# Way in to a batch's experts, an early norm, and silu by tanh in a two-layer Mamba and mixture-of-experts kernel

## The chip, the cores and the metric

The kernel runs on one core of one Trainium2 chip. The metric is the device time of one execution in microseconds (us), as a median over runs. A second set of numbers comes from one execution that was recorded by the hardware profiler.

## The reference

The input is 4 batches of 512 tokens with 256 features. Two layers follow, each a mixer and a mixture of experts. Each of the four parts takes the layernorm of its input and adds the layernorm of its result.

```python
x = x + ln(L0_attn(ln(x)))   # Mamba2-like mixer, 32 heads, state 64, chunks of 128,
                             # then a gated feed-forward of 1024: silu(h @ gate.T) * (h @ up.T) @ down.T
x = x + ln(L0_ffn(ln(x)))    # top 2 of 8 experts, relu(x @ fc)**2 @ proj, weighted by softmax
x = x + ln(L1_attn(ln(x)))   # X = silu(conv(x @ in.T)), gate = sigmoid(x @ g.T), dt = softplus(X . dt_w + dt_b)
                             # s = scan(exp(dt * A), dt * B * X); out = ((C * s + D * X) * gate) @ out.T
x = x + ln(L1_ffn(ln(x)))    # scores = sigmoid(x @ gate.T); top 2 of 8 (scores + bias); xs = score * x in bf16
                             # sum over e: (silu(xs @ w1[e].T) * (xs @ w3[e].T)) @ w2[e].T, plus a shared expert
```

In layer 0 the feed-forward has an RMS norm of its own (norm2) and a residual inside L0_attn. Layer 1's silu stands in three places: behind the conv of the mixer, in the shared expert, and in the eight routed experts.

## The kernel before

Everything runs in one launch. The tokens of a batch are four chunks of 128 (`NC`), and the tiles are 128 partitions high. There are two phases.

In the first, a loop over the batches runs layer 0's mixer, eight head groups for each batch. Beside it, a helper `Side` gives out steps of earlier batches' work. `side.go(us, done)` is called at points of the mixer with the time passed since the last call, and lets the helper run steps of batches before `done` until a share of 0.62 of that time is used. The steps come from generators: `layer0(b)` is the feed-forward of batch b (`feed_forward`) and, for batches 0 and 1, the way into its experts (`experts0_in`), the experts (`experts0_out`) and the way back (`experts0_back`). `side.finish()` behind the loop issues all that is left, one step after the other.

In the second phase new pools are opened, among them buffers of psum: tag `dc` has two of two banks, tag `b` has two. Work is cut into lanes: last feed-forward (of batch 3), `experts0_in`, `experts0_out`, `experts0_back` (for batches 2 and 3), then `mixer1_in`, `mixer1_out`, `experts1_in` and `experts1_out` for all four. A planner picks the next step among the lanes by costs that the steps yield (`yield pe, dve, latency`) and by a rank of the batches, `[2, 3, 0, 1]`. The order that it finds is the program order on each engine, and each engine executes its own in order.

The parts that the change and the steps of the prediction touch, with lines of the kernel before:

- `normed` (L285): RMS norm of a batch by four ACT copies with a scale into `v`, then transposes into `vT` (L135, L139).
- `last_feed_forward`: eight slices of the hidden 1024. Gate and up matmuls (L1003), tanh on ACT (L1005), two DVE steps into `hf` (L1006, L1007), down matmuls (L1012). This one already computes silu as 0.5 * g * (1 + tanh(g / 2)).
- `experts0_in`: layernorm, a copy of the batch to DRAM, transposes into `xT`, router matmuls (L245), top 2 on DVE, counting matmuls (L359, L361) that sort the token slots by expert, places (L380), matmuls that give the tokens of each tile (L403), token numbers (L408) and rows of weights.
- `experts0_out`: 15 tiles (`NT`) of 128 sorted slots. `fetch` gathers tokens `xr` (L441) and expert weights `wx` (L444) by indirect DMAs on POOL's queue, and `three` works on three tiles at a time: transposes of `xr` (L452), first matmul (L459), relu on ACT (L462), square on DVE, second matmul (L467), copy to `yr` (L470), and its DMA to DRAM.
- `experts0_back`: eight gathers on POOL's queue (L494) bring each token's two results back, and ACT and DVE add them up.
- `mixer1_in`: matmul with `w1i` (L1054), conv in four terms (L199 on ACT, L201 on DVE), silu on ACT in place (L1058), gate matmuls and tanh (L1064, L1065), dt as softplus by exp and ln (L209, L212).
- `mixer1_out`: dt rows by DMA, product `uu` on POOL (L1092), exp (L1093) and X times D (L1094) on ACT, scan and two more DVE steps (L1097 to L1099), output matmuls (L1102).
- `experts1_in`: norm, router, top 2 and scores `s`, then the shared expert by `gated` (L1114 matmuls, L1116 silu on ACT, L1117 product on DVE).
- `experts1_out`: for each of four chunks and two halves of the experts, matmuls into a buffer `gu` of tag `dc` (L1164), four silus on ACT with the token's score as scale (L1169), four products on DVE into `he` (L1172). Then transposes (L1183), copies, and the second matmuls with the final layernorm.

The half of `experts1_out` in code:

```python
sg = wk.tile([P, L], F32, tag="s2b", name="sg", bufs=2)
for i in range(4):
    e, o = half * 4 + i, i * P
    S.activation(sg[:, o : o + P], gu[:, o : o + P], AF.Silu, scale=s[:, c, e : e + 1])
for i in range(4):
    e, o = half * 4 + i, i * P
    V.scalar_tensor_tensor(he[:, e, :], gu[:, L + o : L + o + P], s[:, c, e : e + 1],
                           sg[:, o : o + P], ALU.mult, ALU.mult)
```

ACT holds the table of one set of functions at a time; where the next function is of another set, an ACT_TABLE_LOAD stands ahead of it, under the line of that function. In the kernel before, exp (L422) and tanh (L1005) follow each other without one (871.64 and 874.67 us), and silu, exp and ln are each led by one.

Of the kernel before, what the change touches and what calls it, by code (L numbers as in the profile page):

```python
# [37 lines left out]
def tile_layers(  # L38
# [234 lines left out]

    def normed(b, v, vT):

        h1 = h1s[b]
        mv = stats(h1, "a")
        q = small.tile([P, NC], F32, tag="q", name="q")  # L280
        V.tensor_tensor(q, mv[:, :, 0], mv[:, :, 0], ALU.mult)
        V.tensor_tensor(q, q, mv[:, :, 1], ALU.add)
        r = rsqrt(q, "rsa")
        for c in range(NC):
            S.activation(v[:, c, :], h1[:, c, :], AF.Copy, scale=r[:, c : c + 1])  # L285
        yield 0.0, 2.6, 4.0
        transposed(vT, [v[:, c, :] for c in range(NC)], lambda k: cv("norm2", k), "dc")
        yield 1.0, 0.0, 1.8

    def feed_forward(b, beside=True):  # L290

        h1 = h1s[b]
        v = wl.tile([P, NC, DM], F32, tag="v", name="v", bufs=1)
        vT = wl.tile([P, 2, L], F32, tag="vT", name="vT", bufs=1)
        yield from normed(b, v, vT)
        for half in range(2):
            hs, wds = [], []
            for f in range(half * 4, half * 4 + 4):
                we = wst.tile([P, 8, P], F32, tag="wx", name="wf", bufs=5)
                nc.sync.dma_start(out=we[:, 0:2, :], in_=w_gate[:, :, f * P : (f + 1) * P])  # L300
                nc.sync.dma_start(out=we[:, 2:4, :], in_=w_up[:, :, f * P : (f + 1) * P])
                wd = we[:, 4:6, :].rearrange("p a c -> p (a c)")
                nc.sync.dma_start(out=wd, in_=w_down[:, f, :])
                gu = ps("dc", 2)
                gp, up = gu[:, :L], gu[:, L:]
                for i, p in enumerate((gp, up)):
                    for k in range(2):
                        T.matmul(p, we[:, i * 2 + k, :], vT[:, k, :], start=(k == 0), stop=(k == 1))  # L308
                th = wl.tile([P, L], F32, tag="th", name="th", bufs=2)
                S.activation(th, gp, AF.Tanh, scale=0.5)  # L310
                V.scalar_tensor_tensor(th, th, 1.0, gp, ALU.add, ALU.mult)
                hT = wl.tile([P, L], F32, tag="hT", name="hT", bufs=5)
                V.scalar_tensor_tensor(hT, th, 0.5, up, ALU.mult, ALU.mult)  # L313
                hs.append(hT)
                wds.append(wd)
                yield 3.44, 1.5, 0.0
            for c2 in range(2):
                acc = ps("dc", 2)[:, :L]
                for i in range(2):
                    c = c2 * 2 + i  # L320
                    for f in range(4):
                        T.matmul(acc[:, i * DM : (i + 1) * DM], hs[f][:, c * P : (c + 1) * P], wds[f],
                                 start=(f == 0), stop=(f == 3))
                h = h1[:, c2 * 2 : c2 * 2 + 2, :]
                V.tensor_tensor(h, h, rows(acc), ALU.add)
                yield 3.44, 0.7, 0.0
        yield 0.0, 0.0, 0.5
        if beside:
            yield from add_layernorm_by_chunks(b, [h1[:, c, :] for c in range(NC)])
        else:  # L330
            add_layernorm(b, [h1[:, c, :] for c in range(NC)], "a")
        yield 0.0, 4.5, 2.0

    def experts0_in(b, t):
# [8 lines left out]
        V.tensor_copy(lg, router(xT, wr, "dc"))  # L343
        yield 1.8, 0.3, 0.0
        m1, o1 = top1(lg, small, "taa")
        if b < 2:
            yield 0.0, 1.5, 0.3
        l2 = small.tile([P, NC, 8], F32, tag="tla", name="tl")
        V.scalar_tensor_tensor(l2, o1, -3e38, lg, ALU.mult, ALU.add)
        m2, o2 = top1(l2, small, "tba")  # L350
        hot = small.tile([P, NC, 8], BF16, tag="hot", name="hot", bufs=1)
        V.tensor_tensor(hot, o1, o2, ALU.add)
        yield 0.0, 1.9 if b < 2 else 3.4, 0.3

        p = ps("dc", 2)
        sums = p[:, : 5 * 64].rearrange("p (c a e) -> p c a e", a=8, e=8)
# [5 lines left out]
        for c in range(NC):  # L362
# [28 lines left out]
        tl = small.tile([P, 2 * NC, NT], F32, tag="tl15", name="tl15", bufs=1)  # L391
        V.tensor_tensor(tl, partf[:, 1].unsqueeze(2).to_broadcast([P, 2 * NC, NT]),
                        lane[:, :NT].unsqueeze(1).to_broadcast([P, 2 * NC, NT]), ALU.is_equal)
        if b < 2:
            yield 0.0, 1.9, 0.3
        tk = small.tile([P, 2 * NC, 2, NT], BF16, tag="tk", name="tk", bufs=1)
        V.tensor_scalar(tk[:, :, 0, :], tl, mine, None, ALU.mult)
# [109 lines left out]
    def layer0(b, t):  # L507

        yield from feed_forward(b)
        if b < 2:  # L510
            yield from experts0_in(b, t)
            yield from experts0_out(b, t, 0.0)


# [1 line left out]
    with ExitStack() as c1:  # L516
# [369 lines left out]
        for b in range(B):  # L886
# [78 lines left out]
                V.tensor_tensor(h0[:, c2 * 2 : c2 * 2 + 2, :], h0[:, c2 * 2 : c2 * 2 + 2, :], rows(p), ALU.add)  # L965
            side.go(2.0, b + 1)
            t = ahead
        side.finish()


# [4 lines left out]
    def last_feed_forward(b):  # L975
# [9 lines left out]

        wes = [load(f) for f in range(2)]
        yield 0.0, 0.0, 0.0
        v = wl.tile([P, NC, DM], F32, tag="v", name="v", bufs=1)
        vT = wk.tile([P, 2, L], F32, tag="vTf", name="vT", bufs=1)
        yield from normed(b, v, vT)  # L990
        acc = ps("o", 2)
        pend = []
        for f in range(9):
# [43 lines left out]


    D1 = w2.tile([P, 4], F32, tag="D1", name="D1")
    V.tensor_scalar_mul(BC, BC, 0.5)  # L1040
    V.tensor_scalar_mul(D1, col[:, OFF["D1"] : OFF["D1"] + 4], 0.5)

    def mixer1_in(b, t):
        xn = wk.tile([P, NC, DM], F32, tag="xn", name="xn", bufs=2)
        layernorm(b, "m", xn)
        yield 0.0, 2.8, 4.0
        xT = wk.tile([P, 2, L], F32, tag="xTb", name="xT1", bufs=1)
        turned(xT, xn, "b")
        yield 1.0, 0.0, 1.8
        t.X = X = wk.tile([P, 4, L], F32, tag="X", name="X", bufs=2)  # L1050
        for m in range(4):
            p = ps("b")
            for k in range(2):
                i = T.matmul(p, w1i[:, k, m * P : (m + 1) * P], xT[:, k, :], start=(k == 0), stop=(k == 1))  # L1054
                if b + m + k == 0:
                    later(i)
            conv(X[:, m, :], p, lambda t, m=m: cv("cw1", m * 4 + t), cv("cb1", m))
            S.activation(X[:, m, :], X[:, m, :], AF.Silu)  # L1058
            yield 1.72, 2.3, 0.0, (5 if m == 3 else 0)
        t.Gt = Gt = wk.tile([P, 4, L], F32, tag="Gt", name="Gt", bufs=1)  # L1060
        for m in range(4):
            p = ps("b")
            for k in range(2):
                T.matmul(p, w1g[:, k, m * P : (m + 1) * P], xT[:, k, :], start=(k == 0), stop=(k == 1))  # L1064
            S.activation(Gt[:, m, :], p, AF.Tanh, scale=0.5)  # L1065
            yield 1.72, 0.0, 0.0
        dp = ps("b").rearrange("p (c a h) -> p c a h", a=16, h=8)
        for c in range(NC):
            for m in range(4):
                T.matmul(dp[:, c], X[:, m, c * P : (c + 1) * P], repeated(dtw[:, m, :], 16),  # L1070
                         start=(m == 0), stop=(m == 3))
# [37 lines left out]
    def gated(dst, w1, w3, rhs):  # L1109
# [3 lines left out]
            for k in range(2):  # L1113
                T.matmul(p, w[:, k, :], rhs[:, k, :], start=(k == 0), stop=(k == 1))  # L1114
        sg = wk.tile([P, L], F32, tag="s2b", name="sg", bufs=2)
        S.activation(sg, gp, AF.Silu)  # L1116
        V.tensor_tensor(dst, sg, up, ALU.mult)  # L1117

    we1 = {}

# [5 lines left out]
    def experts1_in(b, t):  # L1126
# [8 lines left out]
        t.xb = wk.tile([P, 2, L], BF16, tag="xb", name="xb", bufs=2)  # L1135
        V.tensor_copy(t.xb, xT)
        yield 1.0, 0.7, 1.8
        sc = small.tile([P, NC, 8], F32, tag="lg1", name="sg")
        S.activation(sc, router(xT, fg, "dc"), AF.Tanh, scale=0.5)
        V.tensor_scalar(sc, sc, 0.5, 0.5, ALU.mult, ALU.add)  # L1140
        sel = small.tile([P, NC, 8], F32, tag="sel", name="sel")
        V.tensor_tensor(sel, sc, fb.unsqueeze(1).to_broadcast([P, NC, 8]), ALU.add)
        _, o1, _, o2 = top2(sel, small, "e")
        V.tensor_tensor(o1, o1, o2, ALU.add)
        t.s = small.tile([P, NC, 8], F32, tag="s1", name="s1")
        V.tensor_tensor(t.s, o1, sc, ALU.mult)
        yield 1.8, 4.5, 0.5, 7
        t.hs = wk.tile([P, L], F32, tag="hs", name="hs", bufs=1)
        gated(t.hs, sw1, sw3, xT)
# [1 line left out]

    def experts1_out(b, t):

        xb, s, hs = t.xb, t.s, t.hs
        fw1, fw3, fw2, sw2 = (we1[n] for n in ("fw1", "fw3", "fw2", "sw2"))
        hes = {}

        def inner(c):
            hes[c] = he = wk.tile([P, 8, P], BF16, tag="he", name="he", bufs=3)
            for half in range(2):  # L1160
# [5 lines left out]
                sg = wk.tile([P, L], F32, tag="s2b", name="sg", bufs=2)  # L1166
                for i in range(4):
                    e, o = half * 4 + i, i * P
                    S.activation(sg[:, o : o + P], gu[:, o : o + P], AF.Silu, scale=s[:, c, e : e + 1])  # L1169
                for i in range(4):  # L1170
                    e, o = half * 4 + i, i * P
                    V.scalar_tensor_tensor(he[:, e, :], gu[:, L + o : L + o + P], s[:, c, e : e + 1],  # L1172
                                           sg[:, o : o + P], ALU.mult, ALU.mult)
                yield 1.0, 1.0, 1.4

        def outer(c2):

# [31 lines left out]

    held1 = [Held() for _ in range(B)]
    none = lambda b: iter(())
    stages = [lambda b: last if b == B - 1 else none(b)]
    stages += [lambda b, f=f: f(b, held1[b]) if b > 1 else none(b) for f in (experts0_in, experts0_out, experts0_back)]
    stages += [lambda b, f=f: f(b, held1[b]) for f in (mixer1_in, mixer1_out, experts1_in, experts1_out)]
    N = len(stages)
    rank = [2, 3, 0, 1]
# [123 lines left out]
```

## Time and profile before

| | |
|---|---|
| median of 9 runs | 1286.13 us |
| lowest and highest | 1278.35 and 1294.2 us |
| profiled execution | 1281.69 us |
| its span | 1280.0 us |
| granted TensorE clock | 0.961 of full |
| busy: PE, weight load, DVE, ACT, POOL | 1110.8, 691.7, 793.7, 546.1, 325.3 us |
| ACT_TABLE_LOADs | 63, of 1283 ns each |
| of these before 851 us, 851 to 1061, after 1061 | 25, 11, 27 |

The engines are PE (TensorE's matmuls, with its weight loads apart as PEld), DVE (VectorE), ACT (ScalarE), POOL (GpSimd) and SP (SyncE, which issues DMAs only). A timeline's row gives start, duration, engine, line, operation, output and inputs with their shape, a count, and in brackets the idle time ahead of it with the engine and tile that ended it. A group's row gives a line, the operation, the count, then the busy time, the mean of one in ns, and idle time before.

The last mixer's matmuls end near 860 us. The last feed-forward's gate and up matmuls start at 870.85 us, and it ends at 922.07. From about 1061 us on only layer 1 is left.

### The profile page before, as it was taken

Reading aid. Unit: us, or ns where it says so; the run is one execution under the profiler, and the core shown is the slowest. Engines: PE = TensorE matmul, PEld = TensorE weight load, DVE = VectorE, ACT = ScalarE, POOL = GpSimd, SP = SyncE. Lnnn points to the kernel's source line nnn. Section 1 sums busy time; section 2 is a strip of 40 time slices with the busy share of each in tenths; the row PEclk is TensorE's granted clock in tenths of the full one; section 3 lists DMA queues with packets and bytes.
Section 4 is the critical chain, followed back from the end, with each engine's and each line's share of the span. In section 5 each row is a group of like instructions: output and inputs, shape, how many; then the busy total and the mean of one; then the engine's idle time right before and its main releaser. Section 6 shows DMA issues by size and latency. Waiting matters only on the chain. (4 is left out here: it accounts for less than half of the span.)

```text
span 1280.0 us, 18525 instructions
## 1 busy us (share of the span) xinstructions
PE 1110.8 (87%) x6896; PEld 691.7 (54%) x6896; DVE 793.7 (62%) x1742; ACT 546.1 (43%) x984; POOL 325.3 (25%) x411
## 2 busy tenths in 40 slices
PE   4788888999889899999889999978987697887876
PEld 3344544556546665556556665645656474554543
DVE  6568766656776564767774556743361654876765
ACT  2343432333344434333335433222254556786644
POOL 5021202001214432211134322123234833120200
PEclk9999999999899999999999999989999897999888
DMA  5011010011105453110125440145256552010100
GB/s 157 20 51 34 17 35 18 17 54 34 34 18 166 126 161 108 43 37 19 51 80 157 140 149 25 38 122 176 82 172 185 145 161 74 1 50 1 43 17 25
DMA packets 76153, 97.41 MB, mean 76 GB/s; under 512 B 11008, under 2 KB 62208, under 8 KB 76064
## 3 DMA queue, kind: packets, MB, share of 16 engines
q0 software_dynamic: 13488, 45.10, 12.1%
q1 hardware_dynamic: 53936, 43.26, 11.4%
q10 hardware_dynamic: 8640, 7.87, 1.8%
q8 instruction: 55, 0.90, 0.3%
q14 instruction: 34, 0.28, 0.1%
HBM read 85.25 MB, written 12.12 MB: 76 GB/s over the span
## 5 line engine op out<-in xcount | busy, mean ns | idle before, releaser
L540 PE MATMUL ps_pj<-uT,wg 128*128 128x512 f32 x512 | 256.8, 626 | 9.4 <-ACT bt L698 4.1
L201 DVE SCALAR_TENSOR_TENSOR BT<-ps_pj,col,BT 128x511 f32<-128x511 f32 (+2 forms) x192 | 143.4, 747 | 110.9 <-ACT BT L199 107.5
L719 POOL TENSOR_SCALAR_AFFINE_SELECT sc<-sc 128x1024 f32<-128x1024 f32 x64 | 69.9, 1092 | 460.4 <-DVE sc L716 452.8
L201 DVE SCALAR_TENSOR_TENSOR CT<-ps_pj,col,CT 128x511 f32<-128x511 f32 (+2 forms) x192 | 142.6, 743 | 20.7 <-ACT CT L199 18.1
L540 PEld LDWEIGHTS ps_pj<-uT,wg 128*128 128x128 f32 x512 | 90.6, 194 | 96.1 <-issue 72.3
L199 ACT ACTIVATE CT<-ps_pj,col 128x512 f32<-128x512 f32 x64 | 49.7, 777 | 118.4 <-PE ps_pj L540 118.4
L713 PEld LDWEIGHTS ps_dc<-CT,BT 64*128 64x128 f32 x1024 | 71.0, 190 | 46.5 <-issue 29.3
L713 PE MATMUL ps_dc<-CT,BT 64*128 64x128 f32 x1024 | 89.5, 294 | 7.6 <-DVE sc L716 6.0
L716 DVE TENSOR_TENSOR sc<-sc,ps_dc 128x1024 f32<-128x1024 f32 x64 | 77.7, 1214 | 23.9 <-PE ps_dc L713 21.2
L308 PE MATMUL ps_dc<-vT,wf 128*128 128x512 f32 x192 | 87.9, 597 | 0.7 <-DVE hT L313 0.7
L199 ACT ACTIVATE BT<-ps_pj,col 128x512 f32<-128x512 f32 x64 | 49.7, 776 | 82.9 <-PE ps_pj L540 82.9
L444 POOL DMA_INDIRECT wx<-in_w_exp_dram,wrow x60 | 59.4, 989 | 87.3 <-PE ps_dc L467 38.4
L708 ACT ACTIVATE sc<-ps_dc 128x1024 f32<-128x1024 f32 x64 | 65.6, 1025 | 37.1 <-PE ps_dc L705 36.7
L467 PE MATMUL ps_dc<-wx,hx 128*128 128x256 f32 x240 | 64.8, 395 | 12.5 <-ACT hx L462 11.1
L459 PEld LDWEIGHTS ps_dc<-hx,wx 128*128 128x128 f32 x480 | 61.0, 191 | 18.3 <-issue 9.6
L441 POOL DMA_INDIRECT xr<-XD,token x60 | 58.7, 979 | 42.8 <-PE ps_dc L452 26.9
L459 PE MATMUL ps_dc<-hx,wx 128*128 128x128 f32 x480 | 64.9, 278 | 4.7 <-DMA wx<-in_w_exp_dram,wrow 2.7
L698 ACT COPY bt<-ps_pj 128x384 f32<-128x384 f32 x64 | 30.5, 476 | 77.4 <-PE ps_pj L696 77.4
L463 DVE TENSOR_TENSOR hx<-hx 128x256 f32<-128x256 f32 x60 | 27.4, 458 | 56.7 <-ACT hx L462 56.6
L467 PEld LDWEIGHTS ps_dc<-wx,hx 128*128 128x128 f32 x240 | 43.3, 192 | 30.7 <-ACT hx L462 17.5
L308 PEld LDWEIGHTS ps_dc<-vT,wf 128*128 128x128 f32 x192 | 35.3, 190 | 40.6 <-issue 38.6
L730 PEld LDWEIGHTS ps_pj<-xd,bt 128*128 128x128 f32 x384 | 46.5, 191 | 16.3 <-issue 7.8
(315 smaller groups left out, 2005.9 us busy)
## 6 DMA issues: line engine op xcount, KB each, us to landing
wg<-in_w_in_dram SPq DMA_DIRECT2D x64, 256.0 KB
YS<-yr ACTq DMA_DIRECT2D x60, 128.0 KB
wf<-in_w_gate_dram SPq DMA_DIRECT2D x32, 128.0 KB
wf<-in_w_up_dram SPq DMA_DIRECT2D x32, 128.0 KB
wf<-in_w_down_dram SPq DMA_DIRECT2D x32, 128.0 KB
db<-dD SPq DMA_DIRECT2D x32, 128.0 KB
St<-Mv SPq DMA_DIRECT2D x192, 2.0 KB
x<-in_x_dram SPq DMA_DIRECT2D x4, 512.0 KB
```

What stands on the lines that cost most here:

```text
L199: S.activation(dst, p, AF.Identity, bias=bias, scale=w(3))
L201: V.scalar_tensor_tensor(dst[:, s:], p[:, : L - s], w(3 - s), dst[:, s:], ALU.mult, ALU.add)
L308: T.matmul(p, we[:, i * 2 + k, :], vT[:, k, :], start=(k == 0), stop=(k == 1))
L441: keep(G.indirect_dma_start(out=xr[t], out_offset=None, in_=x, in_offset=bass.IndirectOffsetOnAxis(ap=token[:, t : t + 1], axis=0)))
L444: keep(G.indirect_dma_start(out=ws[t], out_offset=None, in_=w_exp, in_offset=bass.IndirectOffsetOnAxis(ap=wrow[:, t : t + 1], axis=0)))
L459: T.matmul(p[:, L + d * P : L + (d + 1) * P], w[:, k * DM + d * P : k * DM + (d + 1) * P], h[:, k * P : (k + 1) * P], start=(k == 0), stop ...
L467: T.matmul(p[:, 2 * P : 2 * P + DM], h[:, (2 + d) * P : (3 + d) * P], w[:, (2 + d) * DM : (3 + d) * DM], start=(d == 0), stop=(d == 1))
L540: T.matmul(p, w[:, k, :], uT[:, k, :], start=(k == 0), stop=(k == 1))
L708: S.activation(sc, df, AF.Exp)
L713: T.matmul(cb[:, e * L + c * P : e * L + (c + 1) * P], of.BT[e * 64 : (e + 1) * 64, c * P : (c + 1) * P], of.CT[e * 64 : (e + 1) * 64, c * ...
L716: V.tensor_tensor(sc, sc, cb, ALU.mult)
L719: G.affine_select(out=scv, in_=scv, compare_op=ALU.is_ge, fill=0.0, base=0, pattern=[[0, 2 * NC], [1, P]], channel_multiplier=-1)
```

## The change

It has three parts.

1. The way into batch 2's experts (`experts0_in(2)`) is now in `layer0(2)`, behind its feed-forward, among the steps that `side` gives out. It leaves the planner's lanes.
2. `normed` is cut in two. `scaled(b)` holds the statistics and the four ACT copies into `v`. For batch 3 it is issued at once behind the mixer's loop, ahead of `side.finish()`; the transposes stay where they were.
3. In layer 1, silu(g) is computed as 0.5 * g * (1 + tanh(g / 2)): tanh on ACT, then (tanh + 1) * g on DVE. In `mixer1_in` this is one new DVE step for each of four slices of a batch, in `gated` two steps in place of one, in `experts1_out` one new step of 128x512 for each half. The factor 0.5 is folded into BC, D1 and dtw, into the second step of `gated`, and into small tiles of scores `sh` and `s2`. The new tanh tile of `mixer1_in` takes tag `s2b`, whose two buffers `sg` uses too. The planner's DVE costs of the steps are raised.

```diff
-    def normed(b, v, vT):
+    def scaled(b):
         h1 = h1s[b]
+        v = wl.tile([P, NC, DM], F32, tag="v", name="v", bufs=1)
         mv = stats(h1, "a")
...
         for c in range(NC):
             S.activation(v[:, c, :], h1[:, c, :], AF.Copy, scale=r[:, c : c + 1])
+        return v
+
+    def normed(v, vT):
         yield 0.0, 2.6, 4.0
         transposed(vT, [v[:, c, :] for c in range(NC)], lambda k: cv("norm2", k), "dc")
...
         yield from feed_forward(b)
+        yield from experts0_in(b, t)
         if b < 2:
-            yield from experts0_in(b, t)
             yield from experts0_out(b, t, 0.0)
...
+        last_v = scaled(B - 1)
         side.finish()
...
-        yield from normed(b, v, vT)
+        yield from normed(last_v, vT)
...
-    V.tensor_scalar_mul(BC, BC, 0.5)
-    V.tensor_scalar_mul(D1, col[:, OFF["D1"] : OFF["D1"] + 4], 0.5)
+    V.tensor_scalar_mul(BC, BC, 0.25)
+    V.tensor_scalar_mul(D1, col[:, OFF["D1"] : OFF["D1"] + 4], 0.25)
+    V.tensor_scalar_mul(dtw, dtw, 0.5)
...
-            S.activation(X[:, m, :], X[:, m, :], AF.Silu)
-            yield 1.72, 2.3, 0.0, (5 if m == 3 else 0)
+            th = wk.tile([P, L], F32, tag="s2b", name="th1", bufs=2)
+            S.activation(th, X[:, m, :], AF.Tanh, scale=0.5)
+            V.scalar_tensor_tensor(X[:, m, :], th, 1.0, X[:, m, :], ALU.add, ALU.mult)
+            yield 1.72, 3.0, 0.0, (5 if m == 3 else 0)
...
         sg = wk.tile([P, L], F32, tag="s2b", name="sg", bufs=2)
-        S.activation(sg, gp, AF.Silu)
-        V.tensor_tensor(dst, sg, up, ALU.mult)
+        S.activation(sg, gp, AF.Tanh, scale=0.5)
+        V.scalar_tensor_tensor(sg, sg, 1.0, gp, ALU.add, ALU.mult)
+        V.scalar_tensor_tensor(dst, sg, 0.5, up, ALU.mult, ALU.mult)
...
-        t.s = small.tile([P, NC, 8], F32, tag="s1", name="s1")
-        V.tensor_tensor(t.s, o1, sc, ALU.mult)
+        t.sh = small.tile([P, NC, 8], F32, tag="s1", name="sh")
+        V.scalar_tensor_tensor(t.sh, o1, 0.5, sc, ALU.mult, ALU.mult)
+        t.s2 = small.tile([P, NC, 8], F32, tag="s2", name="s2")
+        V.scalar_tensor_tensor(t.s2, t.sh, 2.0, t.sh, ALU.mult, ALU.mult)
...
-                    S.activation(sg[:, o : o + P], gu[:, o : o + P], AF.Silu, scale=s[:, c, e : e + 1])
+                    S.activation(sg[:, o : o + P], gu[:, o : o + P], AF.Tanh, scale=sh[:, c, e : e + 1])
+                V.scalar_tensor_tensor(sg, sg, 1.0, gu[:, :L], ALU.add, ALU.mult)
...
-                    V.scalar_tensor_tensor(he[:, e, :], gu[:, L + o : L + o + P], s[:, c, e : e + 1],
+                    V.scalar_tensor_tensor(he[:, e, :], gu[:, L + o : L + o + P], s2[:, c, e : e + 1],
                                            sg[:, o : o + P], ALU.mult, ALU.mult)
-                yield 1.0, 1.0, 1.4
+                yield 1.0, 2.0, 1.4
...
-    held1 = [Held() for _ in range(B)]
+    held1 = [Held(), Held(), held0[2], Held()]
...
-    stages += [lambda b, f=f: f(b, held1[b]) if b > 1 else none(b) for f in (experts0_in, experts0_out, experts0_back)]
+    stages += [lambda b, f=f, n=n: f(b, held1[b]) if b > n else none(b)
+               for f, n in ((experts0_in, 2), (experts0_out, 1), (experts0_back, 1))]
```

In `experts0_in` three conditions `b < 2` become `b < 3` as well; they are yields that split the top 2 and the last steps for the batches that are given out beside the mixer. In the changed kernel the order of PE's instructions around the last feed-forward is: router, counting matmuls, token matmuls, first transposes of gathered tokens, then that feed-forward's transposes and gate and up matmuls. The eight gathers of batch 2's way back stand on POOL ahead of the first fetches of batch 3's tiles. There are 33 ACT_TABLE_LOADs in it: 25, 2 and 6 in the three parts of the table above.

More of the change, by code (lines that the diff above doesn't have):

```diff
@@ L292, in feed_forward @@
         h1 = h1s[b]
-        v = wl.tile([P, NC, DM], F32, tag="v", name="v", bufs=1)
+        v = scaled(b)
         vT = wl.tile([P, 2, L], F32, tag="vT", name="vT", bufs=1)
-        yield from normed(b, v, vT)
+        yield from normed(v, vT)
         for half in range(2):
@@ L345, in experts0_in @@
         m1, o1 = top1(lg, small, "taa")
-        if b < 2:
+        if b < 3:
             yield 0.0, 1.5, 0.3
@@ L352, in experts0_in @@
         V.tensor_tensor(hot, o1, o2, ALU.add)
-        yield 0.0, 1.9 if b < 2 else 3.4, 0.3
+        yield 0.0, 1.9 if b < 3 else 3.4, 0.3
         p = ps("dc", 2)
@@ L393, in experts0_in @@
                         lane[:, :NT].unsqueeze(1).to_broadcast([P, 2 * NC, NT]), ALU.is_equal)
-        if b < 2:
+        if b < 3:
             yield 0.0, 1.9, 0.3
@@ L987, in last_feed_forward @@
         yield 0.0, 0.0, 0.0
-        v = wl.tile([P, NC, DM], F32, tag="v", name="v", bufs=1)
         vT = wk.tile([P, 2, L], F32, tag="vTf", name="vT", bufs=1)
-        yield from normed(b, v, vT)
+        yield from normed(last_v, vT)
         acc = ps("o", 2)
@@ L1137, in experts1_in @@
         yield 1.0, 0.7, 1.8
-        sc = small.tile([P, NC, 8], F32, tag="lg1", name="sg")
+        sc = small.tile([P, NC, 8], F32, tag="lg1", name="sg", bufs=1)
         S.activation(sc, router(xT, fg, "dc"), AF.Tanh, scale=0.5)
@@ L1152, in experts1_out @@
     def experts1_out(b, t):
-        xb, s, hs = t.xb, t.s, t.hs
+        xb, sh, s2, hs = t.xb, t.sh, t.s2, t.hs
         fw1, fw3, fw2, sw2 = (we1[n] for n in ("fw1", "fw3", "fw2", "sw2"))
```

## The prediction

> **What bounds the kernel now.** I read the page's busy times first, then busy times by stretch of the last 219 us, then the chain of waits there, and last the engines' timelines around 860-1010 us, where the last feed-forward, the way into batch 2's experts and their way back lie.
>
> ```profile
> PE 1110.8 (87%) x6896; PEld 691.7 (54%) x6896; DVE 793.7 (62%) x1742; ACT 546.1 (43%) x984; POOL 325.3 (25%) x411
> ```
>
> TensorE (PE) leads with 87%, and the change takes nothing from it. So a gain must come out of PE's 169 us of idle time, and a loss shows as more of it. 38 us of it lie between 851 and 1061 us, 52.6 us behind 1061. In the stretches of that tail (columns: start:end, length, then busy time of PE, weight load, DVE, ACT, POOL, then clock, DMA share, GB/s):
>
> ```profile
> 1086.20:1119.90 33.70, 28.70 (x117) 16.76 (x117) 30.34 (x75) 25.44 (x48) 4.55 (x4) 0.99 0.00 1
> 1139.40:1174.20 34.80, 31.52 (x127) 18.42 (x125) 30.61 (x78) 20.67 (x40) 7.31 (x5) 1.00 0.03 8
> 1196.70:1228.70 32.00, 25.05 (x120) 15.58 (x120) 26.45 (x77) 19.70 (x47) 5.25 (x5) 0.90 0.05 17
> 1249.20:1280.00 30.80, 19.09 (x105) 10.79 (x103) 16.05 (x59) 13.80 (x41) 1.39 (x2) 0.86 0.08 26
> ```
>
> VectorE (DVE) is 90, 88 and 83% busy in the first three and leaves 3.4, 4.2 and 5.6 us. In the fourth nothing is full: that is one batch's chain alone. The chain of waits shows what ACT's table loads cost there (start, us on the chain, engine, line):
>
> ```profile
> 1093.99 1.28 ACT L1093
> 1096.64 0.89 ACT L1169
> 1100.80 1.28 ACT L1093
> 1104.11 1.28 ACT L1058
> 1122.14 1.28 ACT L209
> 1176.75 1.28 ACT L209
> 1178.29 1.28 ACT L1169
> ```
>
> **Norm of the last feed-forward.** Before, its four copies (L285, 1.70 us from 862.05) stand on ACT ahead of the xT copy at 863.66 that batch 2's router waits for. After, they run behind the mixer, where ACT has 8.16 us idle (851-856). So the router comes 1.7 us sooner: **-1.7**. If that idle time were gone it would be 0.
>
> **Way in.** The words say that batch 2's way in lies beside the mixer. The order of the instructions says otherwise: the steps are given out behind the mixer's last matmul, as before. What moves is their place against the last feed-forward. PE's order becomes router, counting matmuls (L364 after), place matmuls (L408), first transposes of gathered tokens (L457), and only then that feed-forward's transposes and gate/up matmuls. Before, these filled the wait:
>
> ```profile
> 866.06 3.08 PE L245 MATMUL ps_dc<-wr,xT 128*128 128x128 f32 x14 [0.25 <-ACT xT L137]
> 870.85 3.78 PE L1003 MATMUL ps_dc<-vT,wf 128*128 128x512 f32 x8
> 876.76 3.70 PE L1003 MATMUL ps_dc<-vT,wf 128*128 128x512 f32 x8 [1.72 <-DVE hf L1007]
> 898.64 0.38 PE L452 MATMUL ps_dc<-ident,xr 128*128 128x128 f32 x2
> ```
>
> Now PE stands in the chain: router end 868.98-1.7 = 867.3; top-2 on DVE 2.9 (869.18 to 872.06 before); counting 0.5; DVE down to tk 5.55, less two steps of the feed-forward's (2 x 0.69) that lay in it = 4.2; places and token numbers, about 1.9; then POOL (idle before the first fetch, row below) issues weights and tokens, 1.2 each up to the first token gather, and this lands 3.6 us later (page's DMA list). Tokens are there at about 880.7; transposes and vT copies follow, gate/up matmuls start at about 883.5 instead of 870.85. That is 14 us of idle PE, where before 2.7 were idle (0.25, 0.78, 1.72): **+11.3**. What covered the chain before is just the feed-forward; nothing else is left that PE could run there. Bounds: 0, if the matmuls' own waits shrink by as much, and 14.
>
> ```profile
> 878.39 1.07 POOL L444 DMA_INDIRECT wx<-in_w_exp_dram,wrow  x1 [16.38 <-DVE place L380]
> 987.93 1.10 POOL L494 DMA_INDIRECT h<-YS,place  x1 [5.56 <-issue]
> 993.12 0.95 POOL L441 DMA_INDIRECT xr<-XD,token  x1 [0.30 <-issue]
> ```
>
> **What comes back of it.** The experts of batch 2 run seven tiles ahead of where they were, so their way back (eight gathers on POOL's queue, L494) comes sooner against batch 3. Before, those gathers ran among batch 3's fetches (second and third row), and PE stalled:
>
> ```profile
> 996.56 2.08 PE L467 MATMUL ps_dc<-wx,hx 128*128 128x256 f32 x4 [6.29 <-ACT hx L462]
> 1010.86 1.13 PE L467 MATMUL ps_dc<-wx,hx 128*128 128x256 f32 x4 [4.07 <-ACT hx L462]
> ```
>
> With 2.67 for a late weight at 972.5 that is 13.0 us. In the order after, the eight gathers stand on POOL ahead of batch 3's first weights and tokens. That is a new wait: last result to first gather 6.0 (981.9 to 987.9), eight gathers 8 x 1.26 = 10.1, three weights 3.8, one token gather 1.0 and its landing 3.6, together 24.5; behind it batch 3's tiles wait, while PE has about 12.8 us of layer 1's matmuls (L1054, L1064) and the feed-forward's rest: 11 new. Nine table loads go as well (eleven between 851 and 1061, two after), mostly where ACT waits anyway: -1.6 for the one and a quarter that fit a stall. -13.0 + 11.0 - 1.6 = **-3.6** (bounds -10 and +9.4, if the stalls stay).
>
> **Silu by tanh.** Ahead of 1061 us the new DVE steps lie beside idle DVE (1 to 6 tenths busy in the page's slices there): 0. Behind it, 21 of 27 loads go: 21 x 1.283 = 26.9 us of ACT. DVE gains steps whose price stands at like rows:
>
> ```profile
> L1093 ACT ACT_TABLE_LOAD x11 | 14.1, 1283 | 1.9 <-DMA db<-dD 1.7
> L1006 DVE SCALAR_TENSOR_TENSOR hf<-hf,ps_dc 128x512 f32<-128x512 f32 x8 | 5.5, 688 | 21.8 <-ACT hf L1005 21.7
> L1099 DVE SCALAR_TENSOR_TENSOR Gt<-Gt,uu 128x512 f32<-128x512 f32 x16 | 10.8, 683 | 0.1
> ```
>
> L1006 is the same operation as the new step between tanh and he: 32 x 0.688 = 22.0. L1099 has the new X step's shape: the eight behind 1061 cost 5.5. The shared expert's extra step is 4 x 0.69 = 2.8, s2 and the like 0.7: 31 us more DVE, against 69 idle in the tail. Where they fall decides:
> - First stretch: eight halves and a gated step, +6.2; idle DVE takes back 2.2, as 1.2 of its 3.4 us are under 0.1 us each: **+4.0**.
> - Second: +6.2, and 2.5 of its 4.2 idle us lie behind 1166, where they can serve: **+3.7**.
> - Third: +6.2 less 5.55 idle is 0.7, 2.5 if the two cannot mesh; the next dt chain loses the loads at 1176.75 and 1178.29, -2.6: I take the upper end, **-0.1**.
> - Fourth: matmuls, four tanh, the new step, he, and back to one of two buffers of psum. Two halves now take 3.5 us (he starts at 1252.45, 1254.39, 1256.00); with 0.69 more and its wait 4.3. Four pairs: **+3.2**.
>
> Sum +10.8. Bounds: -8.6, if all seven loads on the chain above come off and DVE's gaps take every new step, and +22, if two thirds of the 31 us stay. The new tanh tile of mixer1_in shares two buffers with sg: ACT then waits for DVE to release one, where the silu wrote in place. What is queued behind it on ACT are the conv's first term (L199) and the exps, on which scan and conv wait; 0 to 5, I take 0, since DVE's order puts the step at once behind.
>
> The trace shows loads with no gap behind them: the one at 1100.80 takes 1.28, and the next exp starts at 1102.09. [...]
>
> Speaking against the change: beside POOL's uu (L1092, 1143.99) DVE's L1098 took 1.51 us at 1145.10, and 0.75 at 1099.38. The new X step is of that kind; if all eight of the tail were hit it would be 8 x 0.76 = 6 us more, which I leave to the range. [...]
>
> **Sum.** -1.7 + 11.3 - 3.6 + 10.8 = +16.8. The profiled execution took 1281.69 us (span 1280.0), 4.4 under the median; 1298.5 by it, 1302.9 on the scale of the medians, rounded 1303. A measurement of this kernel tells about 0.5%, 6.4 us, from no change: slower is above 1292.5, faster below 1279.7.
>
> **Rivals.**
> - Faster: ACT's loads, not DVE, bind the tail. For it: the seven loads on the chain, 8.6 us, and 69 us of idle DVE there. Then the tail is -8.6; the way back is free, as batch 2's gathers are over before batch 3 needs POOL (-13 + 4 - 1.6 - 1.7 + 11.3 = -1.0), or better by 5 if the feed-forward, now spread over the experts' tiles, fills their small waits. -10 to -15: 1271 to 1276. It decides if the new steps land in gaps of DVE; against it are three stretches with DVE at 83 to 90%. 0.24.
> - A wash: the way in costs nothing (its lower bound) and half of the tail's 10.8 is absorbed: -1.7 + 0 - 3.6 + 5.4 = 0: within 6.4 us, 1280 to 1292. 0.18.
> - Worse: the stalls of 13.0 us stay with the new wait on top, +9.4 in place of -3.6: +29.8, 1316. 0.08.
> - The words' rival, a way in hidden beside the mixer, is excluded by the order.
>
> The forecast has 0.50, with its own range 1293 to 1312. Slower together 0.58. The range goes from 1271 to 1317 and leaves out some 2 in 10 at the two ends.
>
> **What would show it.** Right: an idle stretch of PE of 10 us or more between router and the first gate/up matmul near 870; the last feed-forward ending at about 946 instead of 922; POOL's eight L499 gathers in one block, with PE waiting for tokens of batch 3 behind it; 33 table loads; DVE above 90% in the stretches between the dt chains of the tail. Wrong: DVE's share there grows by the 31 us while the tail keeps its length or shrinks, or the first gate/up matmul starts before 875.

## The result and the profile after

| | before | after |
|---|---|---|
| median | 1285.68 us (62 runs) | 1314.27 us (20 runs) |
| ratio, 95% interval | | 1.0215 (1.0196 to 1.0234) |
| profiled execution, its span | 1281.69, 1280.0 us | 1310.89, 1309.2 us |
| granted clock | 0.961 | 0.947 |

The change makes the kernel 2.15% slower, 28 us. The forecast was slower, 1303 us, with a range of 1271 to 1317. The page's busy times of after:

```profile
PE 1123.4 (86%) x6896; PEld 698.1 (53%) x6896; DVE 825.2 (63%) x1799; ACT 509.4 (39%) x954; POOL 324.6 (25%) x411
```

DVE has 31.5 us more, where 31 were forecast, and ACT 36.7 less for 30 loads. PE's idle time grew by 16.6 us. PE is also 12.6 us busier with the same 6896 matmuls; the last section comes back to that.

To place the loss I cut the profiled executions at the end of layer 0's last mixer and at the transposes of dts, which end the chain of steps that computes dt for a batch (the dt chain; L253 on PE). The mixer's end is that of its output matmuls (L963), 847.9 us in the profile before; PE's work behind it up to some 860 us is the rest of an earlier batch's feed-forward (L322) and transposes (L135), so "near 860" in the section on the profile before is too late. In us:

| kernel | to the mixer's end | to 2nd dt chain | to 3rd | to 4th | to the end | sum behind the mixer |
|---|---|---|---|---|---|---|
| before | 847.9 | 221.4 | 57.0 | 55.7 | 98.0 | 432.1 |
| after | 852.3 | 226.2 | 63.8 | 53.6 | 113.3 | 456.9 |
| way in and norm | 855.7 | 230.8 | 56.4 | 56.2 | 98.2 | 441.5 |
| silu by tanh alone | 851.3 | 213.6 | 59.9 | 58.4 | 107.3 | 439.2 |
| the same without the DVE steps | 848.9 | 211.5 | 55.5 | 54.9 | 98.7 | 420.5 |
| DVE steps alone | 849.1 | 215.5 | 59.8 | 63.8 | 110.5 | 449.5 |
| planner's costs alone | 853.7 | 213.0 | 60.8 | 63.1 | 100.0 | 436.9 |

Up to the mixer's end the work is the same, and in the profiled executions that end lies between 847.9 and 855.9 us (the run with copies on ACT, further below, has the latter; the one with the exps in one go ran on a slower chip and is left out). The 4.4 us there are within this spread. Behind it, 4.8 us lie ahead of the second dt chain, 20.0 in layer 1's tail; the planner's costs alone also move time from the one into the other (last row). The three stretches of the tail, by the same cuts, after (start:end, length, busy PE, weight load, DVE, ACT, POOL, clock, DMA share, GB/s):

```profile
1078.49:1142.31 63.82, 45.88 (x176) 26.18 (x177) 50.08 (x134) 30.37 (x64) 13.35 (x12) 0.87 0.08 27
1142.31:1195.91 53.60, 46.85 (x220) 28.79 (x220) 44.96 (x124) 28.75 (x63) 10.42 (x8) 0.97 0.10 31
1195.91:1309.20 113.29, 76.94 (x392) 46.92 (x392) 78.23 (x246) 47.98 (x126) 11.93 (x12) 0.85 0.07 24
```

and the same three of before:

```profile
1069.26:1126.29 57.03, 45.58 (x182) 25.93 (x183) 42.80 (x123) 41.45 (x72) 11.11 (x11) 0.90 0.09 26
1126.29:1182.00 55.71, 44.80 (x205) 27.68 (x205) 41.06 (x116) 40.79 (x78) 10.55 (x8) 0.95 0.10 29
1182.00:1280.00 98.00, 72.48 (x388) 45.63 (x388) 63.30 (x217) 49.63 (x122) 11.22 (x12) 0.87 0.09 28
```

The last takes 15.3 us more than before, with 14.9 us more DVE (78.2 against 63.3). ACT has shrunk to 42% there: no bound, but its results now go through one more DVE step.

The way in stands as its order said. PE's timeline of after:

```profile
870.51 2.66 PE L245 MATMUL ps_dc<-wr,xT 128*128 128x128 f32 x14 [0.25 <-ACT xT L137]
876.13 0.29 PE L364 MATMUL ps_dc<-hot,earlier 128*128 128x64 bf16 x2 [2.97 <-DVE hot L357]
881.61 0.39 PE L408 MATMUL ps_dc<-tk,spot 128*128 128x30 bf16 x8 [4.54 <-DVE tk L403]
887.82 0.66 PE L457 MATMUL ps_dc<-ident,xr 128*128 128x128 f32 x2 [5.82 <-DMA xr<-XD,token]
892.73 3.62 PE L1008 MATMUL ps_dc<-vT,wf 128*128 128x512 f32 x8
```

Three waits, 13.3 us together, where before the feed-forward's matmuls ran. Its first gate/up matmul starts 40.4 us behind the mixer's end, 17.5 later than before, and it ends at 953.59. What comes back is in the groups of after, second matmul and token transposes of the experts:

```profile
L472 PE MATMUL ps_dc<-wx,hx 128*128 128x256 f32 x240 | 63.8, 389 | 2.0 <-ACT hx L467 1.9
L457 PE MATMUL ps_dc<-ident,xr 128*128 128x128 f32 x120 | 24.4, 290 | 11.0 <-DMA xr<-XD,token 8.7 <-ACT yr L475 2.3
```

The stalls of 6.29 and 4.07 us are gone (2.0 us idle in all 240, where it was 12.5). The new wait behind the eight gathers cost little; POOL's timeline of after:

```profile
986.63 1.02 POOL L499 DMA_INDIRECT h<-YS,place  x1 [21.52 <-DMA YS<-yr]
996.16 0.95 POOL L499 DMA_INDIRECT yg<-YS,place  x1 [0.30 <-issue]
1001.17 0.96 POOL L446 DMA_INDIRECT xr<-XD,token  x1 [0.30 <-DVE st L113]
```

The gathers stand in one block, and batch 3's first tokens go out at 1001. PE met that with only 1.27 and 0.55 us of waiting, at 1005.98 and 1007.37, as layer 1's matmuls (L1072, L1078) lasted until then.

### The profile page after: what moved, and what is told of

It is laid out like the page before. It is cut to its first block, busy times and chain, and to the rows that moved or that the text cites. A ratio compares the mean times of both kernels' runs of the same rounds, so it can differ in the third digit from the quotient of the medians.

```text
span 1309.2 us, 18517 instructions
## 1 busy us (share of the span) xinstructions
PE 1123.4 (86%) x6896; PEld 698.1 (53%) x6896; DVE 825.2 (63%) x1799; ACT 509.4 (39%) x954; POOL 324.6 (25%) x411
## 5 line engine op out<-in xcount | busy, mean ns | idle before, releaser
L721 DVE TENSOR_TENSOR sc<-sc,ps_dc 128x1024 f32<-128x1024 f32 x64 | 77.7, 1214 | 23.7 <-PE ps_dc L718 21.2
L472 PE MATMUL ps_dc<-wx,hx 128*128 128x256 f32 x240 | 63.8, 389 | 2.0 <-ACT hx L467 1.9
```

The lines of the kernel that those rows point to most:

```text
L472: T.matmul(p[:, 2 * P : 2 * P + DM], h[:, (2 + d) * P : (3 + d) * P], w[:, (2 + d) * DM : (3 + d) * DM], start=(d == 0), stop=(d == 1))
L721: V.tensor_tensor(sc, sc, cb, ALU.mult)
```

## The experiments

The diffs are shortened; "..." stands for lines left out. All runs with silu by tanh but one, and the one with the DVE steps alone, have the planner's raised costs. The first number of each result is the run's median. Ratios are to the kernel before on the same chip, and chips differ (the kernel before took 1285.44, 1286.14, 1285.79 and 1301.06 us on the four that these runs used); so a signed difference in us is the ratio less 1, times 1285.68.

**Way in and early norm.** The lines of parts 1 and 2 in the diff above, without those of part 3.

> The kernel before with the way in and the early norm, silu as before. Theory 1 (the forecast's working: the way in stands in PE's order ahead of the last feed-forward and leaves PE idle, part of it comes back at batch 3): +6.0 us, about 1292, with 10 us or more of idle PE between the router and the first gate/up matmul and the eight gathers of the way back in one block on POOL. Theory 2 (the trace of after puts the first gate/up matmul 17.5 us late, and little comes back): +12 to +18, 1298 to 1304. Theory 3 (the way in costs nothing and the whole loss is silu's): within 3 us of 1286.

1297.04 us, ratio 1.0092 (1.0072 to 1.0112), +11.8. Behind the mixer's end the first gate/up matmul is 16.1 us late (39.1 for 22.9), the second dt chain 9.4, and the stretches of the tail are as before. So this half of the change costs 9.4 us in the trace and 11.8 by the ratio, where 6.0 were forecast. Theory 1 has the idle stretch and the gathers, but its number is too low; theory 2 has the delay and, with +12 at its lower end, nearly the number, but 6.7 us do come back.

**Silu by tanh alone.** The lines of part 3, without the others.

> The kernel before with silu by tanh in all three places, way in and norm as before. Theory 1 (DVE is nearly full in the stretches of the tail, and most of the new steps lengthen them): +10.8 by the forecast, up to +20 by the tail of the trace after, so 1297 to 1306, with DVE over 90% busy between the dt chains. Theory 3 (loads bind): 15 us faster, 1271.

1296.35 us, ratio 1.0102 (1.0076 to 1.0127), +13.1. The time is theory 1's. Its sign, DVE over 90% busy between the dt chains, is not there: 80, 80 and 74% in the three stretches of the tail. The two halves multiply to 1.0195, and after has 1.0215 (from 1.0196): they add up, with no more than a few us between them.

**The loads alone.**

```diff
-            V.scalar_tensor_tensor(X[:, m, :], th, 1.0, X[:, m, :], ALU.add, ALU.mult)
...
-        V.scalar_tensor_tensor(sg, sg, 1.0, gp, ALU.add, ALU.mult)
-        V.scalar_tensor_tensor(dst, sg, 0.5, up, ALU.mult, ALU.mult)
+        V.tensor_tensor(dst, sg, up, ALU.mult)
...
-                V.scalar_tensor_tensor(sg, sg, 1.0, gu[:, :L], ALU.add, ALU.mult)
```

> As the run with silu alone, but the DVE step (tanh + 1) * g is left out in all three places, so tanh stands in for silu: the loads are gone and DVE has what it had. It gives the worth of the loads alone. Theory 1: -8.6 us, the loads on the chain, 1277, and the difference to the run with silu alone is the price of the DVE steps, 19 us or more. Theory 3 (DVE's gaps take the steps): the same time as the run with silu alone.

This kernel leaves out silu's product with g, so its result is another; it is there for its time. 1272.22 us, ratio 0.9894 (0.9859 to 0.9930), -13.6. Against silu alone, 0.9894 to 1.0102 is 27 us for 29 us of DVE work (824.2 busy for 795.1). Theory 3 falls: DVE's idle time takes hardly any of it.

**The DVE steps alone.**

```diff
             S.activation(X[:, m, :], X[:, m, :], AF.Silu)
+            V.scalar_tensor_tensor(X[:, m, :], X[:, m, :], 0.0, X[:, m, :], ALU.mult, ALU.add)
...
+                V.scalar_tensor_tensor(sg, gu[:, :L], 0.0, sg, ALU.mult, ALU.add)
```

> The kernel before with silu kept on ACT and a DVE step of the same shape and operands added in each place (g * 0 + silu, which changes no value): loads as before, DVE as after. It gives the price of the DVE steps alone. Theory 1: +19 us or more, 1305, as nothing is given back; the sum of this and of the run without the steps comes to the run with silu alone within 4 us. Theory 3: within 6 us of 1286.

1301.18 us, ratio 1.0134 (1.0112 to 1.0156), +17.2. The sum with the loads alone would be +3.6; silu alone has +13.1. So the expected sum fails: without the steps the loads are worth 13.6 us, with them 4.1, the latter give or take 4. The run is not quite the steps alone, as it has 68 table loads and not 63 in the order that the planner found. That ACT's removed loads mostly let it deliver sooner to an engine that cannot take it fits, but is not shown.

**The planner's costs alone.**

```diff
-            yield 1.72, 2.3, 0.0, (5 if m == 3 else 0)
+            yield 1.72, 3.0, 0.0, (5 if m == 3 else 0)
...
-                yield 1.0, 1.0, 1.4
+                yield 1.0, 2.0, 1.4
```

> The kernel before with nothing but the planner's two raised costs (3.0 for 2.3 and 2.0 for 1.0), which move steps in program order and leave the work as it is. Theory A (order alone is worth something: in the runs with raised costs the second dt chain comes 6 to 10 us earlier behind the mixer's end than in the kernel before, also where only DVE steps were added): 4 to 8 us faster, 1278 to 1282, with the second dt chain about 215 us behind the mixer's end where it was 221. Theory B (that was the removed loads and chance): within 3 us of 1286.

1286.13 us, ratio 0.9992 (0.9961 to 1.0023): theory B, order is worth nothing in the whole. It does move time: 8.4 us less ahead of the second dt chain, 13.3 more behind it (table). The sum is 4.8 us longer in the trace, which is of the slowest of the ten runs (1292.35 us), and there are 66 table loads for 63. So the early second chain of the runs with these costs is order, not removed loads. The times of the runs above can be read against before; their single stretches cannot, least of all the first two of the tail, which are 11.2 us longer in this trace with nothing changed but the order.

**The early norm alone.** The lines of part 2.

> The kernel before with the early norm alone. The forecast's step: -1.7 us, 1284, the end of the router 1.3 to 1.7 us nearer to the mixer's end (it was 21.2 behind it) and nothing else changed. Rival: what is won ahead of the router is lost again in the waits of batch 3's tiles: 1286.

1286.46 us, ratio 1.0011 (0.9976 to 1.0046). The router ends 19.9 us behind the mixer instead of 21.2, so 1.3 of the 1.7 us are there, and no gain in the whole can be measured.

**Silu by tanh with the old costs.** Part 3 with the two yields left at 2.3 and 1.0.

> Silu by tanh in all three places as in the run with silu alone, but with the planner's costs left at 2.3 and 1.0. Theory A (the raised costs bring 4 to 8 us by order): slower than silu alone by that, 1301 to 1304. Theory B (order matters little): 1296 as silu alone, within 3 us.

1300.95 us, ratio 1.0113 (1.0078 to 1.0149), where silu alone has 1.0102 (1.0076 to 1.0127). By the ratios 1.4 us, which is nearer to theory B, but the two intervals leave room for theory A's 4. What it does settle is the early second chain: with the old costs that stands 222.7 us behind the mixer's end, as before, though 30 loads are gone.

**Copies on ACT in place of DVE's four products.**

```diff
-                V.scalar_tensor_tensor(sg, sg, 1.0, gu[:, :L], ALU.add, ALU.mult)
+                    S.activation(us[:, o : o + P], gu[:, L + o : L + o + P], AF.Copy, scale=s2[:, c, e : e + 1])
+                V.scalar_tensor_tensor(us[:, L:], sg, 1.0, gu[:, :L], ALU.add, ALU.mult)
+                V.tensor_tensor(he[...], us[:, L:], us[:, :L], ALU.mult)   # bf16, 512 wide, one for four
```

> Silu by tanh with another way to he in the routed experts: ACT, which the loads have left, copies the up half with the token's score as scale (four copies of 128x128 a half, 1.14 us), and DVE multiplies twice at 512 wide, the second time with bf16 operands, in place of one step at 512 and four at 128. DVE per half 0.69 + 0.35 to 0.68 for 1.82. Theory 1 (DVE's added steps are what silu by tanh costs in the tail): most of the 24 us between the runs with and without the steps comes back, 1276 to 1284, below the kernel before. Rival (ACT becomes the bound in its place, 36 us more on it): 1292 or more, no better than silu alone.

1297.12 us, ratio 1.0065 (1.0031 to 1.0098). Theory 1 expected 1276 to 1284 and falls; the rival's time came. DVE lost 18.6 us of work against silu alone (of the two products at 512 wide the first took 683 ns, the one in bf16 418), and little came back: 4.7 us by the ratios, which is within their intervals, and in the trace no stretch of the tail is shorter by more than 0.5. The last stretch of silu alone, of this run, and of the next:

```profile
1183.19:1290.50 107.31, 77.13 (x396) 46.41 (x396) 79.28 (x251) 47.25 (x128) 11.23 (x12) 0.85 0.08 25
```

```profile
1187.82:1300.00 112.18, 75.50 (x396) 46.84 (x396) 65.36 (x185) 68.96 (x214) 11.68 (x12) 0.85 0.08 24
```

```profile
1175.96:1275.40 99.44, 73.77 (x396) 44.52 (x396) 74.70 (x243) 47.17 (x125) 11.64 (x12) 0.88 0.08 27
```

Here DVE is 58% busy and the stretch is the longest of the three. DVE's share cannot be what sets it, nor is ACT full, 69 us busy in 112; but the new copies on ACT lie between the matmuls and he, on the same path.

**The DVE step off the path.**

```diff
+                scr = wk.tile([P, L], F32, tag="hf", name="scr", bufs=3)
+                V.scalar_tensor_tensor(scr, hs, 1.0, hs, ALU.add, ALU.mult)   # behind the four products
```

> The run without the DVE steps (tanh stands in for silu), with one DVE step of 128x512 added for each half of the routed experts, but off the path: it reads hs, writes a scratch tile that nobody reads, and stands behind the half's four products. DVE has 22 of the 31 us back, the path from tanh to he has nothing added. Theory chain (the new step costs because it lies between tanh and he, which hold a buffer of psum): within 5 us of the run without the steps, 1272 to 1277, the last stretch about 99 us. Theory occupancy (it costs because DVE is full): about two thirds of the 24 us, 1286 to 1290, the last stretch 104 us or more.

Silu's product is left out here too. 1279.26 us, ratio 0.9946 (0.9919 to 0.9973): 7 us over the run without steps, 20 under silu alone, between what the two theories expected and nearer to the chain's. The last stretch agrees (third row above): 99.4 us with 74.7 of DVE, nearly the length without steps (98.7), where silu alone has 107.3 with 79.3. The kernels whose real work in it is the same and that have no step between tanh and he take 98.7 (without steps), 99.4 (this one) and 100.1 (planner's costs alone) there; the two that have it take 107.3 (silu alone) and 110.5 (DVE steps alone). It is not step for step, though. DVE's order did not follow the place in the code: 16 of the 32 spare steps fall into the last stretch, while silu alone has 22 of its 32 there and two of the shared expert's. From the second dt chain to the end, all 32 steps cost 3.7 us off the path (212.8 for 209.1), and silu alone takes 225.5. The steps of mixer1_in and of the shared expert, 9 of the 31 us, are in silu alone and not in this run; how much of the 20 us is theirs stays open.

What lies on the path shows DVE's timeline of silu alone:

```profile
1223.55 0.66 DVE L1177 SCALAR_TENSOR_TENSOR sg<-sg,ps_dc 128x512 f32<-128x512 f32 x1
1224.19 0.68 DVE L1177 SCALAR_TENSOR_TENSOR sg<-sg,ps_dc 128x512 f32<-128x512 f32 x1
1225.95 1.26 DVE L172 SCALAR_TENSOR_TENSOR x<-ps_o,rso,x 128x256 f32<-128x256 f32 x3
1227.13 1.11 DVE L1180 SCALAR_TENSOR_TENSOR he<-ps_dc,s,sg 128x128 bf16<-128x128 f32 x4
```

and, from PE's, who waits for it:

```profile
1227.52 0.81 PE L1191 MATMUL ps_b<-identb,he 128*128 128x128 bf16 x3 [5.82 <-DVE he L1180]
```

Two visits to DVE for each half instead of one: between them a layernorm of another lane stands in DVE's order, both buffers of psum stay taken, and PE waits 5.8 us. One such row proves little, as before has a wait of 5.4 us for he as well. All waits of PE's transposes for he in the last stretch (us, times, longest), for before, the planner's costs alone, this run, silu alone, and silu with the old costs:

```profile
PE ps_b L1183 <- DVE he L1172: 9.4, 4, 5.4
PE ps_b L1183 <- DVE he L1172: 5.5, 3, 2.9
PE ps_b L1189 <- DVE he L1176: 3.3, 5, 1.6
PE ps_b L1191 <- DVE he L1180: 9.0, 6, 5.8
PE ps_b L1191 <- DVE he L1180: 12.5, 7, 5.1
```

Where the costs are alike, the step on the path adds to them: 3.3 or 5.5 to 9.0 with the raised costs, 9.4 to 12.5 with the old ones.

**Spare matmuls in the waits of the way in.** 5, 8 and 10 of them, in three places.

```diff
+        if b == 2:
+            pf = ps("pj")
+            for i in range(5):
+                T.matmul(pf, xT[:, 0, :P], xT[:, 0, :], start=True, stop=True)
```

> The run with way in and early norm, with 23 spare matmuls of 128x512 on PE that nobody reads, put into the waits of the way in: 5 behind the router, 8 behind the counting matmuls, 10 behind the token matmuls. They change no result and keep PE busy where it stood. Theory clock (the half clock of 876 to 892 us in the trace after comes from PE's idle time, and makes the first matmuls behind it twice as long): clock near 1.0 there, the first gate/up matmul 2 to 4 us earlier behind the router, 1293 to 1295. Rival (the clock has other reasons, or the spare matmuls get in the way of the real ones): 1297 or more, the first gate/up matmul where it was.

1299.91 us, ratio 1.0123 (1.0074 to 1.0171): no gain, the rival's time. Each spare matmul took 0.88 us, so they overran the waits, and the first gate/up matmul came 4.4 us later behind the mixer's end than without them. Whether shorter filling would gain stays open. The timelines still show the clock: from the first token transposes to the first gate/up matmul 4.90 us without them (889.90 to 894.80) and 3.05 with them (892.43 to 895.48), and those eight gate/up matmuls took 4.32 and 3.70 us.

**A mixed version.** Silu on ACT for the last batch's routed experts, and dtw * 0.5 issued late.

```diff
+                    if tail:   # b == B - 1
+                        S.activation(sg[...], gu[...], AF.Silu, scale=sh[:, c, e : e + 1])
...
-    V.tensor_scalar_mul(dtw, dtw, 0.5)
+        if b == 0:   # behind the conv
+            V.tensor_scalar_mul(dtw, dtw, 0.5)
```

> The run with silu by tanh, with two things set right: the routed experts of the last batch keep silu on ACT (beside them runs no exp any more, so it needs one table load), and the product dtw * 0.5 is issued ahead of its first use and not behind the mixer, where DVE waits for its DMA. From the runs: the last stretch 107 to 112 us with the steps and 98 to 100 without, of which the last batch has about half, -4 to -5; the wait for dtw 2.3. Together 1288 to 1290, which is within 0.5% of the kernel before. If loads and steps of the earlier stretches balance better than that, 1283.

1297.39 us, ratio 1.0101 (1.0050 to 1.0151): a miss, no better than silu alone. From the last shared expert (its tanh on ACT) to the end 31.7 us in place of 32.6, but the stretch ahead of it took 78.5 for 74.7. And dtw stands on DVE where it stood, as the order on the engine did not follow the place in the code:

```profile
860.26 0.18 DVE L1063 TENSOR_SCALAR dtw<-dtw 128x32 f32<-128x32 f32 x1 [2.92 <-DMA dtw<-in_dt_w_dram]
```

**Fewer loads without DVE steps.** The kernel before, with the exps of a batch in one go.

```diff
-            S.activation(a[:, m, :], a[:, m, :], AF.Exp, scale=An[:, m : m + 1])
+                for i in range(4):   # at m == 0
+                    S.activation(es[i], a[:, i, :], AF.Exp, scale=An[:, i : i + 1])
```

> The kernel before, silu and all else left as they are, but the four exps of a batch's mixer1_out are issued in one go into tiles of their own (free buffers of the last feed-forward), in place of one at each turn of the loop. 53 table loads in place of 63 and not one DVE step more. From the runs: 21 to 30 loads less were worth 13.6 us where no DVE step was added, so ten are worth 4 to 7: 1279 to 1282. If the four exps in a row keep silu waiting on ACT for as long as the loads took: 1286.

Ratio 1.0008 (0.9981 to 1.0034), 1302.33 us on a chip on which the kernel before took 1301.06. The 4 to 7 us did not come. In the waits of this run's DVE (what waited for whom, us, times, longest) the scan now waits for POOL's product, which the exp used to follow:

```profile
DVE uu L1102 <- POOL uu L1092: 12.1, 7, 2.8
```

That this wait took the place of the loads fits, but no run shows it apart. No version tried here that computes the same result beats the kernel before.

## Why the prediction was right, and where its sum was off

Right were the sign and the mechanism of the way in: PE's idle stretch between router and gate/up matmul, the late end of the last feed-forward (953.6, forecast 946), the gathers in one block, and 33 loads. In the tail the sign was right for a reason that did not hold. The forecast took DVE to be nearly full there, from windows in which it was 83 to 90% busy; between the dt chains it was 75 and 74% busy before and 78 and 84% after, where the forecast named 90% as its sign.

The size was short in both halves: 11.8 us by the ratio for 6.0 in the way in, 13.1 for 10.8 in silu by tanh. 1314 lies in the wide range, but outside the forecast's own 1293 to 1312, and next to the rival "worse" (1316), whose condition, that the stalls stay, did not come true. So that the number lies within the range owes something to luck. The sum was +16.8, the trace shows +24.8 behind the mixer's end. By steps:

- **Norm, -1.7:** 1.3 at the router, nothing in the whole (1.0011).
- **Way in, +11.3:** mis-sized. With the norm it was +9.6; the run has +16.1 at the first gate/up matmul. I took 2.7 us of earlier idle time off, but it lay elsewhere: 0.25 ahead of the router's end, 1.72 behind the start of the gate matmuls. Between tokens and gate matmuls I put 2.8 us; the rows show 4.9, at a granted clock of 0.50. And from the router's end to the tokens I put 13.4 us, where the run took 14.3. That is 5.7 of the 6.5 us.
- **What comes back, -3.6:** -6.7. The stalls went, as said; the new wait, put at 11 us, cost 1.8 on PE.
- **Silu ahead of 1061 us, 0:** nothing to be seen beside the planner's order, but one wait that I had missed: dtw's product stands on DVE ahead of the layernorm on the way to the router and waits for its DMA, 2.71 us in after, and the router ends up to 2.3 us later in the runs with silu by tanh.
- **Tail, +10.8:** +20.0 in after's trace and +14.8 in that of silu alone, but the planner's costs alone put 13.3 us there and change nothing in the whole, so the stretches do not measure this term; the ratio of silu alone does, +13.1. Of the terms inside, one failed by its reason. In the third stretch I let 2.6 us of loads cancel the steps, -0.1; from the fourth dt chain to the last shared expert after took 80.6 us, before 68.8. The loads give little back in the last stretch: 98.7 us without the DVE steps, 98.0 before, 100.1 with the planner's costs alone. In the whole they do not cancel one for one either: loads alone -13.6, steps alone +17.2, both +13.1. The end of the tail looks right, +3.5 for +3.2 from the last shared expert on, but order has a share in that, too: 29.2 before, 30.7 with the planner's costs alone, 32.7 after.
- **Kind of bound:** the forecast charged a step where DVE was nearly full. The run with the step off the path speaks for place more than fullness: 7 us for 22 us of DVE.

The faster rival had its condition half right: the loads were worth 13.6 us, more than the 8.6 on the chain. It fell on the other half, that DVE's 69 idle us would take the steps. The slow X steps beside POOL's uu, which the forecast left to its range, did not come: the sixteen took 674 to 694 ns in after, and only one of them ran beside a uu, for 0.15 us. The shared buffers of the tanh tile, which it left at 0 to 5, were not tried apart.

The run with the loads alone gives 13.6 us for 30 loads, less than the 26.9 that rows of 1283 ns put on 21, so here the row was an upper end. In the trace of before a load stands ahead of each of ACT's 39 changes between silu and exp, and ahead of none of the 17 from exp to tanh.

## What to carry to other kernels

Trading a table load on one engine for a step on another is not settled by busy shares: ask whether the new step lies between a result and the release of its buffer, and how often the path now visits an engine that serves other lanes in order. A step that fills a wait, moved, leaves its wait behind; look in the order of each engine for what will stand there. And price an edit by switching each half off: the loads alone and the steps alone told more than the change did.

## What was not expected of the hardware

PE's idle time is paid twice here. With way in and norm, the granted clock is 0.50 in the waits (first row) and still 0.50 over 4 us in which PE is busy again (second row). With spare matmuls in the waits it is 1.00 in both:

```profile
882.00:888.00 6.00, 0.39 (x8) 0.29 (x8) 1.99 (x6) 0.00 (x0) 4.48 (x6) 0.50 0.74 235
892.00:896.00 4.00, 3.81 (x14) 3.29 (x15) 0.43 (x1) 1.47 (x4) 3.09 (x4) 0.50 0.91 238
```

```profile
882.00:888.00 6.00, 6.00 (x23) 2.70 (x22) 0.36 (x2) 0.00 (x0) 4.35 (x5) 1.00 0.93 324
892.00:896.00 4.00, 3.98 (x28) 3.14 (x27) 0.00 (x0) 2.88 (x6) 1.89 (x2) 1.00 0.56 166
```

That is 2.5 us for the waits of the way in (4.90 to 3.05 and 4.32 to 3.70). How much of PE's 12.6 busier us in after comes from the clock was not tried apart; the tail's L1176 matmuls, 419 ns each for 395 before, make 2.4 of them (37.0 us busy for 34.6). The rows show the two clocks, 0.50 and 1.00, and not when one gives way to the other.
